# Layer 0 experts of a two-layer block: the 64-feature chunk's way down as products over 64 partitions, and both token halves' way down at the end of the step

## The chip, the cores and the metric

The kernel runs on one core of one Trainium2 chip. The metric is the time on the device, in microseconds (us). The core has a matrix engine (TensorE, PE in the profile; its weight loads are PEld), a vector engine (VectorE, DVE), a scalar engine for activation functions (ScalarE, ACT), a general engine (GpSimd, POOL) and an engine that here only issues transfers (SyncE, SP). PE reads SBUF and writes PSUM, which has eight banks; a bank holds 512 numbers of 4 bytes on each of 128 partitions. Everything is computed in 4-byte floats.

## The reference

The input x has shape (4, 512, 256): 2048 tokens of 256 features. Two layers follow each other; each adds an attention branch and a feed-forward branch to x. The change lies in layer 0's feed-forward branch, a gated MLP of 704 hidden features with a low-rank correction by the two best of eight experts:

```python
gate_base = xf @ Wg.T                       # 2048 x 704
up_base   = xf @ Wu.T
base_out  = silu(gate_base) * up_base @ Wd.T
# expert_w: the two largest of softmax(xf @ Wr.T) over 8 experts, else 0
for e in range(8):
    h = silu(gate_base + 2 * xf @ Ag[e].T @ Bg[e].T) * (up_base + 2 * xf @ Au[e].T @ Bu[e].T)
    acc += 2 * h @ Ad[e].T @ Bd[e].T * expert_w[:, e]
out = base_out + acc
```

Layer 0's other branch is a gated recurrent attention (mLSTM) with an MLP of 1024 features; layer 1 has softmax attention over the four batch rows and an MLP with 2-of-4 sparsity. The change does not touch them.

## The kernel before

**Tiling.** The 512 positions are cut in four blocks of 128 (step j = 0 to 3); a block holds 4 x 128 = 512 tokens. `experts(j)` computes the branch above for one block, in two token halves of T = 256 tokens. The 704 features are five chunks of 128 and one of 64. For a chunk and a half, one PSUM bank holds the gate (256 columns) and the up product (256 columns) of 128 features. `products(ps, parts, step)` adds to that bank: step 0 is the base product, steps 1 and 2 add the low-rank terms of the first and the second chosen expert. After each step `gated` makes silu(gate) x up from the bank: ACT's Silu into `sl`, then DVE's product into `hid` (step 0) or into `he` (steps 1 and 2). A bank must have been read before the next step may add to it.

**The 64-feature chunk.** It is done once for both halves (`pair`): half 0's 64 features lie on partitions 0 to 63 of the bank and half 1's on 64 to 127. On the way in, the two halves' products therefore use 64 columns of the PE array each and stand side by side (records with 128*64). The results `hb["pair"]` and `he[0]` (named `he_pair`) have both halves, one above the other.

**The way back.** There are two. The delta: `dps[half]`, a PSUM tile `acc` of 512 columns, sums `adT` x `he` over the chunks; `finish` multiplies it by the routing weights (`tmp`) and adds the two slots to `dw`. The way down: `add_down` sums, over the five chunks, the pair and `dw`, the products of `hid` with `wdT` and of `dw` with `bdT` into one bank `yp` per half, 128 tokens by 256 features twice, and DVE adds it to x. For the pair, `adT` and `wdT` hold the 64 features' rows twice: once on partitions 0 to 63 with zeros below (for half 0), and once on 64 to 127 with zeros above (for half 1). So a product over all 128 partitions of the pair takes only one half's features. POOL writes the zeros at the start (line 370).

**Order of the work.** No engine's order is written out by hand. Every piece of work is a Python generator (a stream); `Flow` runs the stream that is due first by the model `Clock`, which holds a time for each engine, an estimate for each instruction and which PSUM bank is free when. What comes out is a fixed program order for each engine (`InOrder`, line 216, records nearly all operations, so nearly all rows of the profile have that line). `flow.wait` gives control away until something is ready by the model; the hardware's own waits are set by semaphores as the data need them. Beside `experts(j)` run `front(j+1)` (layer norm, transposes, v and gates: `pt`, `vp`), `routing(j+1)` (`lp`, `spread`, `low`), `mlstm(j)` (`q_ps`, `k_ps`, `h_ps`, `r_ps`, `t_ps`, `qk`, `hp`, `o_ps`, then `w_out` and a norm) and `mlp(j-1)` (`gp`, `up`, `w_down`). In step 0 there is no MLP yet. `experts(j+1)` waits with its fourth chunk, and `mlp` with its fifth, for `mixed`, which is set when the step's way down is done.

**PSUM.** Seven banks are shared by all streams (`mm_ps`); the eighth belongs to `acc`. So half 1's delta may begin only when half 0's has been read, and half 0's way down is let into the order then, while half 1's chunks run.

Of the kernel before, what the change touches and what calls it, by code (L numbers as in the profile page):

```python
# [8 lines left out]
F32 = mybir.dt.float32  # L9
AF = mybir.ActivationFunctionType  # L10
ALU = mybir.AluOpType
AX = mybir.AxisListType

P = 128
B, S, D = 4, 512, 256
# [4 lines left out]
DFF = 704  # L20
# [5 lines left out]
AH, ADH = 16, 16  # L26
LOWEST = -3.0e38
FAR = 3.0e4


@with_exitstack
def layers_kernel(ctx: ExitStack, tc: tile.TileContext, io: dict, out: bass.AP):
# [17 lines left out]
    class Clock:  # L50
# [6 lines left out]
        def __init__(self):  # L57
            self.free = dict.fromkeys(("pe", "dve", "act", "pool", "sp", "dma"), 0.8)
            self.spans, self.before, self.rings = {}, {}, {}
            self.banks, self.held = [None] * 7, set()  # L60
            self.table = self.array = None
            self.stalls = []

# [14 lines left out]
            return max(max(s[2], s[3]) for s in spans)  # L78

        def take_bank(self, t):  # L80
            i = min(range(7), key=self.bank_free)
            name = t[:].tensor.name
            if self.banks[i] is not None:
                self.before[name] = self.banks[i]
            self.banks[i] = name

        def room(self, n):

            return sorted(self.bank_free(i) for i in range(7))[n - 1]


        def part(self, ap):
# [95 lines left out]
    def new(pool, shape, tag, bufs=None, dtype=F32):  # L188
        count[0] += 1
        kw = {} if bufs is None else {"bufs": bufs}  # L190
        t = pool.tile(shape, dtype, tag=tag, name=f"{tag}_{count[0]}", **kw)
        clock.ring(t, (id(pool), tag), bufs or (2 if tag in ("xn", "xnT") else 1))
        return t

    def mm_ps(name):
        count[0] += 1
        t = psum.tile([P, 512], F32, tag="mm", bufs=7, name=f"{name}_{count[0]}")
        clock.take_bank(t)
        return t

    def acc_ps():
        return new(psum, [P, 512], "acc", 1)

    class InOrder:

# [83 lines left out]
    def mm(out, lhsT, rhs, start, stop, at_once=1, **kw):  # L289
        array = (lhsT.shape[0], n_of(lhsT))  # L290
        us = 2 * max(0.107, n_of(rhs) * 0.00084) / at_once + 0.1 * (array != clock.array)
        clock.array = array
        clock.issue("pe", "matmul", (out, lhsT, rhs), {}, us)
        pe.matmul(out, lhsT, rhs, start=start, stop=stop, **kw)
# [13 lines left out]
    def load(t, src, by="sp"):  # L308
        dma(t, src, n_of(t) * t.shape[0] * 4 / 0.3e6, by)
        return t  # L310

    def weight(name, n, tag=None, width=None, by="sp"):

        d = io[name]
        kk = d.shape[0] // P
        t = new(wts, [P, width or kk * n], tag or name)[:, 0 : kk * n].rearrange(
            "p (k n) -> p k n", n=n)
        return load(t, d.rearrange("(k p) n -> p k n", p=P), by)
# [35 lines left out]
    for n, name in enumerate(("WgT", "WuT")):  # L354
        load(wguT[:, n, :, :], io[name].rearrange("(k p) n -> p k n", p=P))
    w_og = weight("w_og", D)
    lora = new(wts, [P, 2 * DFF + (NFC + 1) * E * R], "lora")
    bgT = load(lora[:, 0:DFF], io["BgT"])
    buT = load(lora[:, DFF : 2 * DFF], io["BuT"])
    load_x(1)  # L360
    adT = lora[:, 2 * DFF :].rearrange("p (c n) -> p c n", c=NFC + 1)
    wdT = new(wts, [P, NFC + 1, D], "WdT")
    for t, name in ((adT, "AdT"), (wdT, "WdT")):

        whole = DFF // P
        load(t[:, 0:whole, :], io[name][0 : whole * P, :].rearrange("(k p) n -> p k n", p=P))
        for half in range(2):
            mine = slice(half * P // 2, (half + 1) * P // 2)
            other = slice((1 - half) * P // 2, (2 - half) * P // 2)
            nc.gpsimd.memset(t[other, whole + half, :], 0.0)  # L370
            load(t[mine, whole + half, :], io[name][whole * P : DFF, :])
    bdT = load(new(wts, [P, D], "BdT"), io["BdT"])
    mh_c = column("mh_w")
    w_out = weight("w_out", D)
# [98 lines left out]
    with ExitStack() as l0:  # L473
# [5 lines left out]
        def tmp():  # L479
            return new(wk0, [P, 512], "tmp", 7)  # L480
# [410 lines left out]
        def add_down(xb, bp, terms):  # L891

            yield from flow.wait(banks=1)
            yp = mm_ps("yp")
            for i in range(2):
                for n, (a, lo, w) in enumerate(terms):
                    if n % 4 == 0 and i == 0:
                        yield from flow.wait(*(t[0] for t in terms[n : n + 4]))
                    elif n % 4 == 0:
                        yield 0  # L900
                    mm(yp[:, i * D : (i + 1) * D], a[:, lo + i * P : lo + (i + 1) * P], w,
                       start=(n == 0), stop=(n == len(terms) - 1))
            xv = xb[:, bp : bp + 2, :].rearrange("p b d -> p (b d)")
            dve.tensor_tensor(xv, yp, xv, ALU.add)
# [64 lines left out]
        def experts(j):  # L969
# [12 lines left out]
            def slots(t):  # L982
                return t.rearrange("p (s n) -> p s n", s=K_TOP)

            def here(half):
                return slice(half * T, (half + 1) * T)
# [42 lines left out]
                    yield flow.soon(0.2)  # L1029

            rooms, hb, he, dps = {}, {}, {}, {}
            ended = set()

            def finish(half, t):
                yield from flow.wait(dps[half])
                dve.tensor_tensor(t, dps[half], t, ALU.mult)
                dw = new(wk0, [P, T], "dw", 1)
                dve.tensor_tensor(dw, slots(t)[:, 0, :], slots(t)[:, 1, :], ALU.add)
                ended.add(half)
                terms = [(hb[half, c], 0, wdT[:, c, :]) for c in range(last)]  # L1040
                yield from add_down(
                    xb, 2 * half, [*terms, (hb["pair"], 0, wdT[:, last + half, :]), (dw, 0, bdT)])
                if half == 1:
                    mixed.add(j)

            def base(i):
                yield from flow.wait(xnT, *(wguT[:, m, :, :] for m in range(2)), banks=1)
# [20 lines left out]
            for i in range(len(order) + 4):  # L1068
                if i < len(order) and i not in rooms:
                    yield from base(i)  # L1070

                    while j not in lows and len(rooms) < 4:
                        yield from base(len(rooms))
                    while j not in lows:
                        yield flow.soon()
                    low, wT = lows[j]
                if i == len(order) - 1:
                    based.add(j)
                if i == 3:
                    while j > 0 and j - 1 not in mixed:  # L1080
                        yield flow.soon()
                for step in (1, 2):
                    n = i - step
                    if not 0 <= n < len(order):
                        continue
                    if step == 1:
                        he[n] = new(wk0, [P, 512], "he_pair") if n == 0 else tmp()
                    yield from unread(n)
                    yield clock.over(rooms[n])
                    yield clock.ready(*(low[m][:, step - 1, :] for m in range(2)))  # L1090
                    products(rooms[n], order[n], step)
                    gated(n, rooms[n], slots(he[n])[:, step - 1, :])
                    if step == 2:
                        flow.add(freed(n))
                        if n == len(order) - 1:
                            spent.add(j)
                n = i - 4
                if 0 < n < len(order):
                    _, half, c = order[n][0]
                    if c == 0:  # L1100
                        while half == 1 and 0 not in ended:
                            yield flow.soon()
                        dps[half] = acc_ps()
                        weight = tmp()
                        for s in range(K_TOP):
                            dve.tensor_scalar(
                                slots(weight)[:, s, :], wT[:, here(half)],
                                (-LORA_SCALE, LORA_SCALE)[s], 0.0, ALU.mult, ALU.max)
                        yield clock.over(dps[half])
                    yield from unread(n)  # L1110
                    yield clock.ready(he[n])
                    mm(dps[half], adT[:, c, :], he.pop(n), start=(c == 0), stop=False)
                    if c == last - 1:
                        yield from unread(0)
                        yield clock.ready(he[0])
                        mm(dps[half], adT[:, last + half, :], he[0], start=False, stop=True)
                        flow.add(finish(half, weight), after=True)

        def main():
            for j in range(NJ):  # L1120
# [36 lines left out]
        flow.until(lambda: not flow.streams)  # L1157


    qkvT = weight("qkvT", 3 * D, "WdT", (NFC + 1) * D)  # L1160
    f_gate = weight("f_gate", FF, "wguT", 4 * DFF)
    f_up = weight("f_up", FF, "lora", 2 * DFF + (NFC + 1) * E * R)
    f_down = weight("f_down", D, "w_gate")
    aoT = weight("aoT", D, "w_out")

# [221 lines left out]
```

## Time and profile before

| | |
|---|---|
| median of 3 runs | 798.95 us (798.55 to 799.13) |
| the profiled execution | 798.61 us |
| its span, first to last instruction | 796.9 us |
| PE busy | 779.3 us (98%) |
| DVE, ACT, POOL busy | 409.1, 258.1, 166.1 us |
| granted TensorE clock | 1.00 throughout |
| layer 0 to layer 1 | about 560 us into the span |

A row of a group has the line, engine, operation, the tile written and the tiles read, the shape, how often, and then busy time and the mean duration of one. For a matmul, "128*128" are partitions and columns of the PE array that it uses. A matmul of 4-byte floats appears as two records. Records of matmuls overlap, so their pace is read from start to start. A row in order of time has the start and the duration of a run of equal records, and in brackets how long the engine had stood idle before it and for whom. A row of waits has who waited for whom, the sum, how often, and the longest.

### The profile page before, as it was taken

Reading aid. Unit: us, or ns where it says so; the run is one execution under the profiler, and the core shown is the slowest. Engines: PE = TensorE matmul, PEld = TensorE weight load, DVE = VectorE, ACT = ScalarE, POOL = GpSimd, SP = SyncE. Lnnn points to the kernel's source line nnn. Section 1 sums busy time; section 2 is a strip of 40 time slices with the busy share of each in tenths; the row PEclk is TensorE's granted clock in tenths of the full one; section 3 lists DMA queues with packets and bytes.
Section 4 is the critical chain, followed back from the end, with each engine's and each line's share of the span. In section 5 each row is a group of like instructions: output and inputs, shape, how many; then the busy total and the mean of one; then the engine's idle time right before and its main releaser. Section 6 shows DMA issues by size and latency. Waiting matters only on the chain.

```text
span 796.9 us, 8736 instructions
## 1 busy us (share of the span) xinstructions
PE 779.3 (98%) x3334; PEld 536.2 (67%) x3334; DVE 409.1 (51%) x943; ACT 258.1 (32%) x462; POOL 166.1 (21%) x153
## 2 busy tenths in 40 slices
PE   6999999999999999999999999999999999999998
PEld 3678776876657687864778876655645485664486
DVE  5685545773531676452156433221256883975870
ACT  3454316461231545212156212111243405224310
POOL 5230160600510240060011040000233213342000
PEclk9999999999999999999999999999999999999999
DMA  8820000200000300000030012001000000000000
GB/s 264 275 75 1 1 0 13 96 1 1 0 1 0 107 1 1 1 0 1 0 107 1 1 67 92 1 0 53 0 1 0 1 18 10 1 24 4 0 27 27
DMA packets 18938, 25.37 MB, mean 32 GB/s; under 512 B 2768, under 2 KB 12752, under 8 KB 18896
## 3 DMA queue, kind: packets, MB, share of 16 engines
q1 hardware_dynamic: 17776, 24.27, 9.4%
q10 hardware_dynamic: 1120, 0.54, 0.2%
q8 instruction: 26, 0.43, 0.2%
q14 instruction: 16, 0.13, 0.1%
HBM read 22.65 MB, written 2.16 MB: 31 GB/s over the span
## 4 chain that ended last, share of the span: by engine, by line
PE 96%; DVE 2%; ACT 1%; issue 1%; POOL 0%; POOLq 0%; DVEq 0%; ACTq 0%
PE yp L216 24%; PE chunk L216 19%; PE gp L216 14%; PE up L216 14%; PE acc L216 5%; PE qk_ps L216 3%; PE hp L216 3%; PE pt L216 2%; PE vp L216 2%; PE o_ps L216 2%; PE v_ps L216 2%; PE lp L216 2%; PE qk L216 1%; PE q_ps L216 1%; PE h_ps L216 1%; PE st_ps L216 1%
## 5 line engine op out<-in xcount | busy, mean ns | idle before, releaser
L216 PE MATMUL chunk<-low,lora 128*128 128x256 f32 (+1 forms) x384 | 87.4, 385 | 2.8 <-DVE tmp L216 2.8
L216 ACT ACTIVATE sl<-chunk 128x256 f32<-128x256 f32 x132 | 48.3, 384 | 120.3 <-PE chunk L216 113.0
L216 PE MATMUL chunk<-xnT,wguT 128*128 128x256 f32 (+1 forms) x384 | 84.2, 383 | 0.0
L216 PEld LDWEIGHTS chunk<-xnT,wguT 128*128 128x128 f32 (+1 forms) x384 | 63.7, 181 | 17.7 <-issue 6.0
L216 PEld LDWEIGHTS chunk<-low,lora 128*128 128x128 f32 (+1 forms) x384 | 63.1, 181 | 17.7 <-issue 4.0
L216 ACT ACT_TABLE_LOAD x44 | 56.5, 1283 | 21.1 <-PE chunk L216 15.8
L216 DVE TENSOR_TENSOR hid<-up,tmp 128x512 f32<-128x512 f32 x32 | 22.1, 691 | 78.1 <-PE up L216 75.4
L216 PE MATMUL gp<-featT,w_gate 128*128 128x512 f32 x128 | 60.2, 593 | 0.0
L216 PE MATMUL gp<-xnT,wguT 128*128 128x512 f32 x128 | 60.2, 592 | 0.0
L216 PE MATMUL up<-featT,w_up 128*128 128x512 f32 x128 | 60.2, 592 | 0.0
L216 PE MATMUL up<-xnT,lora 128*128 128x512 f32 x128 | 60.1, 592 | 0.0
L216 DVE TENSOR_TENSOR x<-yp,x 128x512 f32<-128x512 f32 x24 | 16.6, 691 | 83.3 <-PE yp L216 83.3
L216 PE MATMUL yp<-w_gate,hs 128*128 128x256 f32 x256 | 56.2, 379 | 0.0
L216 PE MATMUL yp<-w_down,hid 128*128 128x256 f32 x256 | 56.1, 379 | 0.0
L216 PEld LDWEIGHTS yp<-w_down,hid 128*128 128x128 f32 x256 | 48.6, 190 | 8.3 <-issue 1.7
L216 PEld LDWEIGHTS yp<-w_gate,hs 128*128 128x128 f32 x256 | 48.6, 190 | 6.6
L216 ACT ACTIVATE tmp<-gp 128x512 f32<-128x512 f32 x32 | 19.1, 597 | 101.3 <-PE gp L216 101.3
L216 PE MATMUL yp<-WdT,hid 128*128 128x256 f32 x192 | 46.3, 384 | 0.0
L216 PEld LDWEIGHTS up<-xnT,lora 128*128 128x128 f32 x128 | 24.3, 190 | 29.8 <-issue 29.7
L216 PEld LDWEIGHTS gp<-featT,w_gate 128*128 128x128 f32 x128 | 24.2, 190 | 28.8 <-issue 28.2
L216 PEld LDWEIGHTS up<-featT,w_up 128*128 128x128 f32 x128 | 24.1, 190 | 27.5 <-issue 27.3
L216 PEld LDWEIGHTS gp<-xnT,wguT 128*128 128x128 f32 x128 | 23.9, 190 | 27.4 <-issue 26.5
(198 smaller groups left out, 1211.3 us busy)
## 6 DMA issues: line engine op xcount, KB each, us to landing
ct<-m_dram SPq DMA_DIRECT2D x8, 1024.0 KB, 8.0
out<-x SPq DMA_DIRECT2D x8, 256.0 KB, 2.1
x<-in_x SPq DMA_DIRECT2D x3, 512.0 KB, 10.1
w_gate<-in_w_gate SPq DMA_DIRECT2D x1, 1024.0 KB, 6.0
w_up<-in_w_up SPq DMA_DIRECT2D x1, 1024.0 KB, 7.3
w_down<-in_w_down SPq DMA_DIRECT2D x1, 1024.0 KB, 10.7
wguT<-in_f_gate SPq DMA_DIRECT2D x1, 1024.0 KB, 4.9
lora<-in_f_up SPq DMA_DIRECT2D x1, 1024.0 KB, 5.0
```

The lines of the kernel that those rows point to most:

```text
L216: return tc.keep_in_program_order(f(*args, **kw))
```

## The change

`adT` and `wdT` lose the sixth slice and the zeros: the 64 features' rows stand twice in one slice, on partitions 0 to 63 and on 64 to 127. The products with the pair take 64 partitions each, half 0's on the upper and half 1's on the lower, issued one directly behind the other and written to two banks. For the delta this means that `dps[0]` and `dps[1]` must be open at once: the private bank goes, all eight are shared, half 0's delta ends with the pair, and half 1's begins with it. For the way down both halves' banks `yps` are taken together after half 1's delta. Half 0's `finish` only makes its `dw` (two buffers now); half 1's does the pair for both halves, then half 0's chunks and `dw`, then half 1's. `mixed` is set at the same place, the end. The routing weights are scaled after a half's last chunk instead of before its first. The scheduler makes a new order from this for every engine.

```diff
+BANKS = 8
...
-    def acc_ps():
-        return new(psum, [P, 512], "acc", 1)
...
-    adT = lora[:, 2 * DFF :].rearrange("p (c n) -> p c n", c=NFC + 1)
-    wdT = new(wts, [P, NFC + 1, D], "WdT")
+    adT = lora[:, 2 * DFF :].rearrange("p (c n) -> p c n", c=NFC)
+    wdT = new(wts, [P, NFC, D], "WdT")
     for t, name in ((adT, "AdT"), (wdT, "WdT")):
         whole = DFF // P
         load(t[:, 0:whole, :], io[name][0 : whole * P, :].rearrange("(k p) n -> p k n", p=P))
         for half in range(2):
-            mine = slice(half * P // 2, (half + 1) * P // 2)
-            other = slice((1 - half) * P // 2, (2 - half) * P // 2)
-            nc.gpsimd.memset(t[other, whole + half, :], 0.0)
-            load(t[mine, whole + half, :], io[name][whole * P : DFF, :])
+            load(t[half * P // 2 : (half + 1) * P // 2, whole, :], io[name][whole * P : DFF, :])
...
             def finish(half, t):
                 yield from flow.wait(dps[half])
                 dve.tensor_tensor(t, dps[half], t, ALU.mult)
-                dw = new(wk0, [P, T], "dw", 1)
+                dw = dws[half] = new(wk0, [P, T], "dw", 2)
                 dve.tensor_tensor(dw, slots(t)[:, 0, :], slots(t)[:, 1, :], ALU.add)
-                ended.add(half)
-                terms = [(hb[half, c], 0, wdT[:, c, :]) for c in range(last)]
-                yield from add_down(
-                    xb, 2 * half, [*terms, (hb["pair"], 0, wdT[:, last + half, :]), (dw, 0, bdT)])
-                if half == 1:
-                    mixed.add(j)
+                if half == 0:
+                    return
+                yield from flow.wait(banks=2)
+                yps = [acc() for _ in range(2)]
+
+                def down(half, i, a, w, stop=False, **kw):
+                    mm(yps[half][:, i * D : (i + 1) * D], a[:, i * P : (i + 1) * P], w, stop=stop,
+                       skip_group_check=True, **{"start": False, **kw})
+
+                for i in range(2):
+                    for half in range(2):
+                        down(half, i, hb["pair"][mine[half], :], wdT[mine[half], last, :],
+                             start=(i == 0), at_once=2)
+                for half in range(2):
+                    for i in range(2):
+                        yield 0
+                        for c in range(last):
+                            down(half, i, hb[half, c], wdT[:, c, :])
+                    yield from flow.wait(dws[half])
+                    for i in range(2):
+                        down(half, i, dws[half], bdT, stop=(i == 1))
+                    xv = xb[:, 2 * half : 2 * half + 2, :].rearrange("p b d -> p (b d)")
+                    dve.tensor_tensor(xv, yps[half], xv, ALU.add)
+                    released(yps[half])
+                mixed.add(j)
...
-                    mm(dps[half], adT[:, c, :], he.pop(n), start=(c == 0), stop=False)
-                    if c == last - 1:
-                        yield from unread(0)
-                        yield clock.ready(he[0])
-                        mm(dps[half], adT[:, last + half, :], he[0], start=False, stop=True)
-                        flow.add(finish(half, weight), after=True)
+                    mm(dps[half], adT[:, c, :], he.pop(n), start=((half, c) == (0, 0)),
+                       stop=((half, c) == (1, last - 1)))
+                    if c < last - 1:
+                        continue
+                    if half == 0:
+                        yield from unread(0)
+                        yield from flow.wait(he[0], banks=1)
+                        dps[1] = acc()
+                        for h in range(2):
+                            mm(dps[h], adT[mine[h], last, :], he[0][mine[h], :], start=(h == 1),
+                               stop=(h == 0), at_once=2)
+                    weight = tmp()
+                    for s in range(K_TOP):
+                        dve.tensor_scalar(
+                            slots(weight)[:, s, :], wT[:, here(half)],
+                            (-LORA_SCALE, LORA_SCALE)[s], 0.0, ALU.mult, ALU.max)
+                    released(dps[half])
+                    flow.add(finish(half, weight), after=True)
```

## The prediction

> **What bounds the kernel now.** I read the page first, then TensorE's waits, its groups with their shapes kept apart, and its instructions in order of time.
>
> ```profile
> span 796.9 us, 8736 instructions
> ...
> PE 779.3 (98%) x3334; PEld 536.2 (67%) x3334; DVE 409.1 (51%) x943; ACT 258.1 (32%) x462; POOL 166.1 (21%) x153
> ```
>
> TensorE (PE) is idle for 796.9 - 779.3 = 17.6 us. Who is waited for:
>
> ```profile
> PE pt L216 <- DVE xn L216: 7.6, 1, 7.6
> PE chunk L216 <- DVE tmp L216: 2.8, 3, 1.5
> PE hp L216 <- DVE ct L216: 1.6, 2, 0.9
> PE h_ps L216 <- ACT qs L216: 1.3, 3, 0.5
> PE yp L216 <- ACT oT L216: 0.2, 1, 0.2
> ```
>
> That is 13.5 us; the other 4 lie behind the last product. 7.6 us are the start. So the time is the sum of PE's work plus some 6 us of small waits, and only these two can move. The groups that the change touches:
>
> ```profile
> L216 PE MATMUL yp<-WdT,hid 128*128 128x256 f32 x192 | 46.3, 384 | 0.0
> ...
> L216 PE MATMUL acc<-he_pair,lora 128*128 128x512 f32 x16 | 8.4, 608 | 0.0
> ```
>
> A matmul makes two records. The 384 and 608 ns are latencies; what counts is the pace, from start to start. In the first stretch below, eight records of `chunk<-xnT,wguT` at 256 columns take 305.89 - 304.17 = 1.72, so 0.216 a record. At 512 columns it is 0.43 (`acc`, two records from 304.17 back to 303.31).
>
> ```profile
> 304.17 1.89 PE L216 MATMUL chunk<-xnT,wguT 128*128 128x256 f32 x8
> 305.89 1.03 PE L216 MATMUL chunk<-low,lora 128*128 128x256 f32 x4
> 306.85 1.17 PE L216 MATMUL qk<-qm,kT 32*128 32x128 f32 x32
> 307.95 1.13 PE L216 MATMUL chunk<-low,lora 128*128 128x256 f32 x4
> 308.92 0.97 PE L216 MATMUL hp<-va,ct 128*128 128x33 f32 x8
> ```
>
> ```profile
> 118.18 1.89 PE L216 MATMUL chunk<-xnT,wguT 128*128 128x256 f32 x8
> 120.00 1.08 PE L216 MATMUL chunk<-low,lora 128*64 128x256 f32 x8
> 121.01 1.99 PE L216 MATMUL chunk<-xnT,wguT 128*128 128x256 f32 x8
> 122.84 1.04 PE L216 MATMUL pt<-ident,xn 128*128 128x128 f32 x8
> ```
>
> These show how small products run side by side: `qk` (32 partitions, four at once, each into its own bank) does 32 records in 1.10 us, and the pair chunk (64 columns of the array, two at once) does 8 in 1.01, where one after the other they would need 3.5 and 1.73. They also show what a change of the array's shape costs, if the groups on both sides are counted in. First stretch: 308.92 - 305.89 = 3.03, against 2 x 0.864 for the `chunk` groups and 0.87 for eight slots of 128 columns (the eight transposes from 59.80 to 60.67): 0.43 over. Second: 4.66 against 1.73 + 0.86 + 1.73: 0.34 over.
>
> **The change, part by part.** (1) Delta of the 64-feature chunk, `acc<-he_pair`. Removed per step j: two products over 128 partitions, half of them zeros, 4 records x 0.43 = 1.72. Added: two over 64 partitions side by side, 2 slots x 0.43 = 0.86. (2) Its way down, `yp<-WdT`: removed four products, 8 x 0.216 = 1.73; added four over 64 partitions in two banks, 4 slots = 0.86. No row shows 64 partitions x 128 columns. The bounds of the price of such an excursion are 0.34 (columns split) and 0.43 (partitions split); I take 0.43, since `qk` splits partitions and loads 128 columns of weights per tile as the new products do. So each group gains 0.864 - 0.43 = 0.43, and four steps of two groups gain 3.5 us.
>
> Here the Trainium skill speaks against the row. Page "TensorE: Matmul & The Clock Gate", section "Measured speedup vs the span model", has 3.07x for four row tiles at 512 columns, 77% of the ideal. For two tiles I estimate 1.53x from that: 3.45 us a step become 2.25, a gain of 1.2, or 4.8 us in all. Page "TensorEngine Tiling (Array Packing)", section "Key Properties", says that a change of the tiling mode drains the array: a price per excursion, not per column. The trace agrees with that one and gives its size (0.43 around `qk`, whose tiles otherwise keep the pace of one). My groups are short and stand alone, so I take the trace: 3.5.
>
> (3) In the built order, two new groups stand directly beside another split group: in step 0 the way down follows `chunk` of the pair (64 columns), in step 1 it follows `qk`. One change of shape is saved in each, about half of 0.43: 0.4 us together (bounds 0 and 0.86). PE's work: -3.9 us.
>
> (4) Half 0's whole way down is moved behind half 1's last delta: 24 records of WdT, 4 of BdT (28 x 0.216 = 6.05 us of PE work, of which the pair's part is priced above), and DVE's `x<-yp,x` of 0.69. The amount is the same, but it was filler between `hp` and `qk` and is now missing there; experts chunks stand there instead. Worked out against the built order:
>  - Step 1, after `qk`. `hp` waited 0.86 and 0.76 because it stood right behind `qk`; now `gp` (1.72) and nine WdT products (over 3 us) stand between. Gain 1.6.
>  - Tail of step 0. The wait of 1.54 at 97.46 was for DVE's gated product, late because ACT ran the tanh of `o_ps` and a Square of 0.95 before the Silu. `o_ps` now comes after the tail, with `hp` among the chunks. From the `qk` before, DVE has four `ct` (2.6), a `tmp<-pr` and the gating (0.42 each) plus hand-overs, about 3.8 us; PE has 1.94 + 0.86 + 0.81 = 3.6, and a second such place is about as close. I charge 0.4 and gain 1.54.
>  - Behind `yp<-w_out` of step 0, the way down (4.3 us of cover in the old order) is gone: PE reaches the pair's second low-rank product 1.07 + 1.83 + 0.86 = 3.8 us later, while DVE does `xn` (0.69), a gate (0.42), four statistics (0.53 each) and two small ones before `he_pair` (0.42): 4.3, plus 0.2 to hand over. New wait 0.7. Queued behind it on PE: step 1's chunks, and the transposes of `xn`.
>  - Step 1 between `r_ps` and `t_ps`: the layer norm of the next row block now stands ahead on DVE (three statistics 1.7, four small ops 0.7) of `tmp<-chunk`, for which PE's low-rank product waits: about 0.75.
>  - Half 0's `x` addition (0.69) now stands on DVE ahead of `ss`, which POOL's `qm` (2.34) and the transposes `pt<-ident,qm` wait for. `qm` is ready about 16.3 us after `spread` ends (o_ps 3.45, tanh, Square, reduction, POOL's 5.44 us power, `ss`, `qm`); PE has 16.9 us of work before it. Hidden by half 1's ten WdT products; without them 0.7.
> Waits: -3.2 + 1.9 = -1.3 us. Steps 2 and 3 have MLP products as filler around the change and the same order from `q_ps` to `t_ps`: nothing.
>
> (5) The four memsets on POOL (0.80 to 1.89 us) go, so `ident` is ready 1.1 us earlier. Nothing is won: DVE's first statistics start at 3.38, when the first x lands (issued 0.80, fastest landing 2.6). If x came earlier, 0.5. SP's loads keep number, sizes and order, except that two loads for layer 1 change places; the last of them is issued at 487 and layer 1's products read from 565 on. The second `dw` buffer and the eighth shared bank are not a cost: one bank was the delta's own, and two are held only at the end of a step. The masks' scaling (`tmp<-wT`, 0.29 each) moves behind the deltas; `dw` is read ten products later.
>
> Sum: -3.9 - 1.3 = -5.2 us on the profiled execution of 798.61 (span 796.9 and 1.7 around it): 793.4. The median of the runs shown is 0.34 above that execution: 793.8.
>
> **The rivals.** (a) *The waits just go*: the four new waits don't come. -3.9 - 3.2: 791.8; with excursions at 0.34, 0.7 less, 791.1. For it: with over 98% busy, the planner found cover nearly everywhere. Against: the two DVE queues above. (b) *The waits come back elsewhere*: new waits eat all of the 3.2 and half of the gain in work: about 797. For it: steps 0 and 1 have little filler, and the old order had three waits for gating there. (c) *No overlap*: products over 64 partitions go one after the other. The work stays, excursions cost 8 x 0.43 - 0.4, the waits win 1.3: 800.7. Against: `qk` overlaps four tiles, 6 to 7 ns apart in start. (d) *Slower, the filler is missing*: in step 0 no MLP runs yet, and the way down of half 0 covered `ct<-qk` on DVE (0.68 each, 15.2 us waited in all) between `hp`. The chunks in its place need ACT and DVE (0.38 + 0.42) for each product and DVE is in their way. If all 6.05 us are uncovered in step 0 and half in step 1, 9.1 us: 802.9. It is slower than before once more than 5.2 us beyond my 1.9 stay uncovered. Against: the order puts 8 products of chunks and `lp` (3.4 us) there, and the waits that I find are below 1 us.
>
> **How the numbers follow.** Forecast 0.46, (a) 0.17, (b) 0.17, (c) 0.07, (d) 0.13. What a measurement can tell from no change is 0.2%, 1.6 us: faster is below 797.35, slower above 800.55. Faster: forecast, (a) and (b), 0.80. (c) lies at the upper edge and is halved, and of (d) a third ends within: same 0.07, slower 0.13. Range: from (a) at 0.34 an excursion, 791.0, to 798.0 past (b); the outside is (c), (d) and little else.
>
> **What would show it.** PE's busy time near 775.5 us; `he_pair` records in twos 6 ns apart and the group with its neighbours at 1.3 us against 1.72; no wait of `hp` for `ct`; waits for `tmp` and `he_pair` of about 2 to 3 us in all (with the 0.63 and 0.68 at 35 and 58, whose order is unchanged); 7.6 at the start. Wrong if the new groups take as long as the old, or if PE's idle time in the first 250 us grows by more than 3 us.

## The result, and the profile after

| | before | after |
|---|---|---|
| median | 798.84 us (798.28 to 799.81) | 792.87 us (792.41 to 793.17) |
| the profiled execution | 798.61 us | 792.43 us |
| its span | 796.9 us | 790.7 us |
| PE busy | 779.3 us | 775.3 us |
| PE idle in the span | 17.6 us | 15.4 us |

The ratio of the times is 0.9923, with a 95% interval of 0.9911 to 0.9936: the changed kernel is faster by 6.0 us. The granted TensorE clock is 1.0 in both.

The page of the changed kernel, its span and its busy times:

```profile
span 790.7 us, 8729 instructions
...
PE 775.3 (98%) x3334; PEld 530.7 (67%) x3334; DVE 407.4 (52%) x943; ACT 260.6 (33%) x464; POOL 166.6 (21%) x149
```

The span is 6.2 us shorter. PE's busy time gives 779.3 - 775.3 = 4.0 of it, PE's idle time 17.6 - 15.4 = 2.2. PE is still the bound at 98%.

PE's waits after: who waited for whom, the sum, how often, the longest.

```profile
PE pt L214 <- DVE xn L214: 7.8, 1, 7.8
PE h_ps L214 <- ACT qs L214: 1.5, 3, 0.5
PE chunk L214 <- DVE tmp L214: 1.3, 2, 0.7
PE st_ps L214 <- issue: 0.4, 1, 0.4
PE yp L214 <- ACT oT L214: 0.2, 1, 0.2
PE chunk L214 <- DVE he_pair L214: 0.2, 1, 0.2
```

The wait of `hp` for `ct` (1.6 us in all) is gone, and of the three waits of `chunk` for `tmp` the longest, 1.5. Two small ones are new: `st_ps` and `he_pair`. The sum is 11.4 us, against 13.5.

PE's groups with their shapes kept apart, the two that now use 64 partitions (line, engine, tiles, shape, records | busy us, mean ns | idle before):

```profile
L214 PE MATMUL acc<-WdT,hid 64*128 64x256 f32 x32 | 4.5, 402 | 0.0
L214 PE MATMUL acc<-he_pair,lora 64*128 64x512 f32 x16 | 4.5, 641 | 0.0
```

The number of records is the same, 192 for the way down and 16 for the delta; 32 and all 16 of them now use 64 partitions. The delta's 8.4 us of busy time are 4.5; each record is longer (641 ns against 608), but they overlap in twos.

What such a group costs is read from start to start. Step 1's delta in order of time:

```profile
165.58 1.02 PE L214 MATMUL acc<-tmp,lora 128*128 128x512 f32 x2
166.53 1.13 PE L214 MATMUL acc<-he_pair,lora 64*128 64x512 f32 x4
167.59 1.99 PE L214 MATMUL chunk<-xnT,wguT 128*128 128x256 f32 x8
169.42 1.89 PE L214 MATMUL chunk<-low,lora 128*128 128x256 f32 x8
```

From 165.58 to 169.42 it is 3.84 us. At full pace the three groups need 0.86 (two records at 0.43), 0.86 (two slots at 0.43) and 1.73 (eight records at 0.216), 3.45 together. So the excursion to 64 partitions costs 0.39: about 0.09 before the group, 0.20 within it and 0.10 behind it.

### The profile page after: what moved, and what is told of

Same layout as the page of the kernel before. It is cut to its first block, busy times and chain, and to the rows that moved or that the text cites. A ratio compares the mean times of both kernels' runs of the same rounds, so it can differ in the third digit from the quotient of the medians.

```text
span 790.7 us, 8729 instructions
## 1 busy us (share of the span) xinstructions
PE 775.3 (98%) x3334; PEld 530.7 (67%) x3334; DVE 407.4 (52%) x943; ACT 260.6 (33%) x464; POOL 166.6 (21%) x149
## 4 chain that ended last, share of the span: by engine, by line
PE 95%; DVE 2%; issue 1%; ACT 1%; DMA 0%; POOL 0%; DVEq 0%; ACTq 0%
PE chunk L214 18%; PE yp L214 18%; PE gp L214 14%; PE up L214 14%; PE acc L214 11%; PE qk_ps L214 3%; PE hp L214 3%; PE pt L214 2%; PE vp L214 2%; PE o_ps L214 2%; PE lp L214 2%; PE v_ps L214 2%; PE qk L214 1%; PE q_ps L214 1%; PE st_ps L214 1%
## 5 line engine op out<-in xcount | busy, mean ns | idle before, releaser
L214 DVE TENSOR_TENSOR x<-yp,x 128x512 f32<-128x512 f32 x16 | 11.0, 690 | 68.9 <-PE yp L214 68.9
L214 PE MATMUL acc<-WdT,hid 128*128 128x256 f32 (+1 forms) x192 | 41.3, 386 | 0.0
```

Of the source, the lines that this page charges most:

```text
L214: return tc.keep_in_program_order(f(*args, **kw))
```

## The experiments

E1, E2 and E4 have the instructions of the changed kernel in the same order (E4 but for the order of four products), so they separate what the products do from what the order does.

**E1: the order alone.** Every product with the pair goes over 128 partitions again. The stationary rows are the 64 features' twice, so it also adds the other half's features; only the amount of work is meant. `rows` tells the planner to reckon with 64, so that it makes the same order.

```diff
-    def mm(out, lhsT, rhs, start, stop, at_once=1, **kw):
-        array = (lhsT.shape[0], n_of(lhsT))
+    def mm(out, lhsT, rhs, start, stop, at_once=1, rows=None, **kw):
+        array = (rows or lhsT.shape[0], n_of(lhsT))
...
-                        down(half, i, hb["pair"][mine[half], :], wdT[mine[half], last, :],
-                             start=(i == 0), at_once=2)
+                        down(half, i, hb["pair"], wdT[:, last, :],
+                             start=(i == 0), at_once=2, rows=P // 2)
...
-                            mm(dps[h], adT[mine[h], last, :], he[0][mine[h], :], start=(h == 1),
-                               stop=(h == 0), at_once=2)
+                            mm(dps[h], adT[:, last, :], he[0], start=(h == 1),
+                               stop=(h == 0), at_once=2, rows=P // 2)
```

> The changed kernel with every engine's order kept instruction for instruction, but the products with the pair over all 128 partitions again (each takes the features of both halves, so this part of the result is another; only the time is read). It separates the new order from the products side by side. Theory (the side-by-side products save 0.864 us less some 0.40 for the change of the array's shape, twice a step, with 0.4 us more where two shapes adjoin: about 4.0 us; the new order gives the other 2 us in waits): 796.8 us, PE busy near 779.3, waits as in the changed kernel (11.4 us). Rival 1 (the order does it all, the products gain nothing): 792.9. Rival 2 (the order gives nothing, the products all 6 us): 798.8.

Measured: 796.54 us (796.45 to 797.52), against 798.86 before on the same chip; ratio 0.9972 (0.9961 to 0.9983). PE's busy time is 779.2 us, that of before, and its waits are those of the changed kernel (7.9, 1.5, 1.3, 0.4, 0.2 and 0.2 us).

So the new order is worth 798.86 - 796.54 = 2.3 us with no product narrowed, and narrowing them is worth 796.54 - 792.87 = 3.7 (the kernel before took 798.86 and 798.84 us beside the two).

**E2: the delta narrowed, the way down not.** Of E1's edit, only the way down's part.

> As before, but only the pair's way down over 128 partitions; the delta stays over 64 (the way down takes the features of both halves, another result for this part; only the time is read). Order kept. Theory (each group gains its 0.864 less the price of one change of shape, and the way down gains 0.4 more in the two steps where it stands beside another split group): delta 4 x 0.46 = 1.85, way down 4 x 0.46 + 0.4 = 2.25, so 792.87 + 2.25 = 795.1 us. Rival (the price per change is so high for the short way down that only the delta gains): 793.0. Rival (the longer products of the delta gain nothing): 796.8.

Measured: 794.84 us (793.96 to 795.73), ratio 0.9945 (0.9932 to 0.9958). By the medians the delta is worth 796.54 - 794.84 = 1.7 us, the way down 794.84 - 792.87 = 2.0.

**The same sums without the start.** A median of five or six executions carries the start of the program with it, and the start varies. The same 16 `vp` products, in the changed kernel's profile and in E2's:

```profile
9.97 5.08 PE L214 MATMUL vp<-wvg,xnT 128*128 128x280 f32 x16
10.09 6.19 PE L214 MATMUL vp<-wvg,xnT 128*128 128x280 f32 x16
```

The first of these records follow each other every 0.467 us, the later ones every 0.236. The pace changes at about 12.1 us in the one and 14.5 us in the other, where the trace's record of the granted clock goes to 1.0. Behind that, a kernel repeats itself closely. From the first `spread` to the start of the last group (`yp<-w_gate,hs`, 64 records), with the later experiments beside:

| profile | us |
|---|---|
| before | 757.34 |
| E1 | 755.21 |
| E2 | 753.13 |
| changed kernel; E10 (the same kernel again); E4 | 751.03; 751.03; 751.04 |
| E3 | 752.46 |
| E6 | 755.60 |
| E7; E11 (the same kernel again) | 749.92; 749.91 |
| E9 | 748.56 |

So the order is worth 2.1 us, the delta 2.1 and the way down 2.1, together 6.3. The medians' 1.7 for the delta is low by less than the start can move a single execution (`vp` takes 4.82 us in E1's profile and 6.19 in E2's).

**E4: does the order within a group matter?** The way down issues half 0's two products with the pair, then half 1's two, where the changed kernel alternates. Neighbours in the program then use the same 64 partitions.

```diff
-                for i in range(2):
-                    for half in range(2):
+                for half in range(2):
+                    for i in range(2):
```

> The changed kernel with the four products of the pair's way down in another order: both of half 0's first, then both of half 1's, so that a product has a neighbour on the other 64 partitions only at the seam. If records start strictly in order (theory), half 0's second record pair holds back half 1's first: of 8 records only those at the seam overlap, 7 places instead of 4, 3 x 0.216 = 0.65 us a step, 2.6 us in all: 795.5 us. If PE starts whatever has its 64 partitions free (rival), 792.9. In between, 794.2, if one matmul's two records can be passed by the next matmul's.

Measured: 792.62 us (792.01 to 793.27), ratio 0.9922 (0.991 to 0.9934): as fast as the changed kernel. The theory behind 795.5, products started strictly in the program's order, falls. In E4's order of time, step 2:

```profile
334.32 5.66 PE L214 MATMUL acc<-WdT,hid 64*128 64x256 f32 x28
339.81 1.03 PE L214 MATMUL acc<-BdT,dw 128*128 128x256 f32 x4
```

and in the changed kernel's:

```profile
334.49 5.65 PE L214 MATMUL acc<-WdT,hid 64*128 64x256 f32 x28
339.97 1.03 PE L214 MATMUL acc<-BdT,dw 128*128 128x256 f32 x4
```

A row is named by its first record's shape, so `64*128 ... x28` is eight records of the pair and twenty of half 0's chunks. From its start to `BdT` it is 5.49 and 5.48 us. Half by half in strict order, the two halves could only have met at the seam, seven slots in place of four: 0.65 us more. In the single records of E4 they start in twos all the same, 14 ns apart, four times. The records don't show which 64 partitions they use; that the two of each pair lie on different halves is inferred from the time that the group takes.

**E3: the price of an excursion.** The pair's products for the second 128 tokens come later, behind half 0's chunks for the first: the same products, one trip to 64 partitions and back more in each step.

```diff
-                for i in range(2):
+                def pair_down(i):
                     for half in range(2):
                         down(half, i, hb["pair"][mine[half], :], wdT[mine[half], last, :],
                              start=(i == 0), at_once=2)
+                pair_down(0)
                 for half in range(2):
                     for i in range(2):
                         yield 0
                         for c in range(last):
                             down(half, i, hb[half, c], wdT[:, c, :])
+                        if (half, i) == (0, 0):
+                            pair_down(1)
```

> The pair's way down of each step is divided: its products for the first 128 tokens of each half come first as before, those for the second 128 come behind half 0's five chunks for the first. TensorE so goes over to 64 partitions and back once more in each of the four steps; the number and the length of the products stay. If a trip costs by itself, 0.40 us as measured where the pair's products stand in the changed kernel, the time is 792.9 + 4 x 0.40 = 794.5. If the 0.40 belongs to the place and not to the trip (the first products of a group waiting for something else), it is 792.9.

Measured: 794.57 us (793.99 to 794.85), ratio 0.9945 (0.9933 to 0.9958). That is 1.7 us above the changed kernel, 0.43 a trip; without the start 752.46 - 751.03 = 1.4, 0.36 a trip. The waits are the same (11.3 us), PE's busy time is 776.9 against 775.3. The same place in E3's order of time:

```profile
335.41 6.05 PE L214 MATMUL acc<-WdT,hid 64*128 64x256 f32 x28
341.29 1.03 PE L214 MATMUL acc<-BdT,dw 128*128 128x256 f32 x4
```

28 records take 5.88 us here and 5.48 there: 0.40. The price belongs to the trip, not to the number of products. It also says where narrowing stops to pay: two products of 256 columns side by side save 0.43 us and cost about 0.40.

**E6: is it the held-back way down that removes the waits?** The delta as changed; each half's way down by `add_down` over 128 partitions as soon as its `dw` is there, as before.

```diff
+                terms = [(hb[half, c], 0, wdT[:, c, :]) for c in range(last)]
+                yield from add_down(
+                    xb, 2 * half, [*terms, (hb["pair"], 0, wdT[:, last, :]), (dw, 0, bdT)])
-                if half == 0:
-                    return
-                yield from flow.wait(banks=2)
-                yps = [acc() for _ in range(2)]
...
```

> The pair's delta as in the changed kernel (64 partitions, side by side, both halves at the end of half 0), the way down as in the kernel before: each half's own products over 128 partitions as soon as its weights are there, half 0's between half 1's chunks. (The rows of the pair's way down hold both halves' features here, so the sum that it makes is not the layer's.) By the other runs the delta side by side is worth 1.7 us, so 797.1 if all of the order's 2.3 us comes from holding half 0's way down back to the end, and 794.9 if it comes from moving the delta product of half 1 away from the tail. Theory: the tail's 1.5 us goes with the delta, the two waits of hp for ct stay: 795.6 to 796.2.

The edit also moves the scaling of the routing weights back ahead of a half's first chunk.

Measured: 797.12 us (796.35 to 797.98), ratio 0.9979 (0.9971 to 0.9987). The theory falls, and the first alternative holds: of the 1.8 us gained, 1.7 are the delta's, and the order gives nothing (without the start E6 gains 1.7, less than the delta's 2.1). The tail of step 0 in E6:

```profile
91.08 3.62 PE L214 MATMUL o_ps<-w_og,xnT 128*128 128x256 f32 x16
94.54 1.89 PE L214 MATMUL chunk<-low,lora 128*128 128x256 f32 x8
96.27 1.02 PE L214 MATMUL acc<-tmp,lora 128*128 128x512 f32 x2
98.83 1.13 PE L214 MATMUL chunk<-low,lora 128*128 128x256 f32 x4 [1.54 <-DVE tmp L214]
```

It is the wait of before, of the same length, though the pair's delta has left the tail. In the changed kernel the low-rank products of the last chunks come before `o_ps`:

```profile
82.32 0.98 PE L214 MATMUL hp<-va,ct 128*128 128x33 f32 x8
83.13 1.11 PE L214 MATMUL chunk<-low,lora 128*128 128x256 f32 x4
84.07 1.02 PE L214 MATMUL acc<-tmp,lora 128*128 128x512 f32 x2
```

With half 0's way down held back, the planner had nothing else to put between the `hp` groups and put the last chunks there. What used to stand there becomes the filler behind `o_ps`, and PE waits for none of it. The place of the scaling isn't what does it: E7 below scales ahead of the first chunk in step 0, holds the way down back, and has no wait in the tail. One reservation: the planner gives E6 another order in step 1 too, so E6 shows what the tail's wait depends on, not what each `hp` wait does; there one of the two came back (0.8 us).

**E5: one trip per step.** Can the price be paid once? Half 0's delta stays open until the end of half 1; there both halves' products with `he_pair` and the pair's way down stand together.

```diff
-                    mm(dps[half], adT[:, c, :], he.pop(n), start=((half, c) == (0, 0)),
-                       stop=((half, c) == (1, last - 1)))
-                    if c < last - 1:
+                    mm(dps[half], adT[:, c, :], he.pop(n), start=(c == 0), stop=False)
+                    if (half, c) != (1, last - 1):
                         continue
...
+                    yield from unread(0)
+                    yield from flow.wait(he[0], banks=2)
+                    yps = [acc() for _ in range(2)]
+                    for h in range(2):
+                        mm(dps[h], adT[mine[h], last, :], he[0][mine[h], :], start=False,
+                           stop=True, at_once=2)
+                    for b in range(2):
+                        for h in range(2):
+                            down(yps, h, b, hb["pair"][mine[h], :], wdT[mine[h], last, :],
+                                 start=(b == 0), at_once=2)
```

> Half 0's delta is kept open until half 1's end, so that the pair's two delta products and its four products of the way down stand together: one change of the array's shape a step instead of two (the masks' scaling for both halves at half 1's last chunk). Theory (price of a change 0.40 us): four changes fewer, 1.6 us, but in two steps the way down loses its neighbour of another split shape or gains one (0.2 each way): 791.3 us, if the waits stay. In its order step 0 has three groups of hp directly behind qk, where PE should wait for ct on DVE (4 x 0.68 us): 0.8 to 1.5 us back, so 792.1 to 792.8. Rival (the price of a change is small and the gain of the changed kernel was less overlap than order): 793 to 794.5.

Measured: 793.58 us as a median, ratio 0.9933 (0.9914 to 0.9952), but the six times are two values: 791.83, 791.65, 791.31 with a mean granted clock of 1.0, and 795.60, 795.33, 795.68 with 0.996. The lower value lies between the two that were expected; the upper was expected by nobody. The profiled execution is one of the upper. PE's order of time there, in step 0:

```profile
81.19 1.17 PE L214 MATMUL qk<-qm,kT 32*128 32x128 f32 x32
83.13 3.87 PE L214 MATMUL hp<-va,ct 128*128 128x33 f32 x24 [0.76 <-DVE ct L214]
86.81 2.05 PE L214 MATMUL chunk<-low,lora 128*128 128x256 f32 x4
88.65 3.34 PE L214 MATMUL acc<-tmp,lora 128*128 128x512 f32 x4
```

and the same time in two stretches (the stretch, its length, the busy time and instructions of PE, PEld, DVE, ACT and POOL, then the granted clock, the DMA share and GB/s):

```profile
81.35:84.76 3.41, 2.65 (x47) 2.46 (x47) 2.38 (x4) 0.00 (x0) 0.00 (x0) 1.00 0.00 0
84.76:91.59 6.83, 6.83 (x20) 4.88 (x20) 4.27 (x16) 0.39 (x1) 1.84 (x3) 0.50 0.00 1
```

For 6.8 us TensorE runs at half its clock: four `chunk` records take 1.84 us in place of 0.86. Half of 6.8 is 3.4 us lost, and the two values lie 795.6 - 791.65 = 3.9 apart; the other 0.5 is within what the start moves. Ahead of the fall stand four things in a row: `qk` on 32 partitions, a wait of 0.76, and three `hp` groups of 33 columns each, which the changed kernel has apart, with wide products between.

**E8: a wide product ahead of each `hp` group.** E5, with a product that nothing reads put before step 0's last four `hp` groups.

```diff
                 hp = mm_ps("hp")
+                if first and s == 1:
+                    mm(hp[:, D : 2 * D], wq[:, 0, :], w_og[:, 1, :], start=True, stop=True)
```

> The one-trip kernel with a useless product of 256 columns over 128 partitions ahead of each of step 0's last four hp groups (it writes columns of the bank that nothing reads). It adds 4 x 0.43 = 1.7 us of products and covers up to 0.8 us of the first hp's wait. If three hp groups of 33 columns in a row are what halves the granted clock, it stays at 1.0 in every execution and the time is 791.6 + 1.7 - 0.8 = 792.5, up to 793.3, without a second value. If the clock falls for another reason (the wait, the phase of the step, a power limit that large products raise), about half of the executions are 4 us longer again, at 796 to 797.

Measured: 794.25 us, 793.62 to 794.41 in five executions, ratio 0.994 (0.9926 to 0.9953), with a clock of 0.999 or more in each. There is no second value, as expected. The time is 1 us above the upper end of the expectation: the added product waited for `ct` as well and covered nothing, and the planner moved other work about.

```profile
83.16 0.70 PE L214 MATMUL hp<-w_og,wq 128*128 128x256 f32 x2 [0.77 <-DVE ct L214]
83.69 0.97 PE L214 MATMUL hp<-va,ct 128*128 128x33 f32 x8
84.50 0.68 PE L214 MATMUL hp<-w_og,wq 128*128 128x256 f32 x2
```

and the 3.4 us around the first of them, in the form of E5's stretches:

```profile
81.50:84.92 3.42, 2.65 (x44) 2.39 (x41) 2.51 (x5) 0.00 (x0) 0.00 (x0) 1.00 0.00 0
```

Only two `hp` groups follow the wait here before a chunk, not three. So `qk` and the wait alone don't bring the clock down; the kernel before, with `qk` and a wait of 0.86 us in step 1, says the same. PE's busy share isn't what decides either: it is 2.65 us in this stretch as in E5's stretch just before the fall.

**E7: the mixed kernel.** Step 0 with two trips, steps 1 to 3 as in E5; in step 0 a half's masks are scaled with its first chunk.

```diff
+                    if j == 0:
+                        if (half, c) == (0, 0):
+                            yield from flow.wait(banks=1)
+                            dps[0] = acc()
+                        if c == 0:
+                            weight = tmp()
...
+                        continue
```

> Step 0 close to the changed kernel (two trips to 64 partitions), steps 1 to 3 with one trip: half 0's delta stays open, and both halves' last delta products and the pair's way down stand together at the end of half 1. Three trips fewer at 0.40 each, and no three hp groups in a row in step 0: 792.9 - 1.2 = 791.7, at a granted clock of 1.0 throughout. If one-trip steps lose as much again to late masks, 792.9; if the clock falls here too, 795 to 796 in some executions.

Measured: 791.65 us (790.81 to 792.23), ratio 0.9909 (0.9896 to 0.9923), the clock at 0.999 or more in each. As expected.

**E9, E10, E11: the clock once more, and the lead.** E9 is E7 with half 0's and half 1's masks in step 0 scaled one chunk later (`if c == 1`), which gives another order in step 0. E10 is the changed kernel, E11 is E7, all on one chip.

> The mixed kernel with half 0's masks scaled one chunk later, which moves step 0's products: three hp groups of 33 columns stand in a row again, but a chunk and a delta product of full width stand between the qk group and them. If three hp groups in a row halve the granted clock, it falls in about half of the executions and the time has two values about 4 us apart (792 and 796). If it takes the narrow qk group, the wait and the three hp groups together, the clock is 1.0 in every execution and the time is one value, 791.5 to 793.

> The changed kernel beside the mixed one on the same chip: 792.9, and so 1.2 us above the mixed kernel if that one's lead is real, equal to it if the lead came from the chip.

> The mixed kernel once more, beside the changed one on the same chip: 791.7.

Measured: E9 790.93 us (789.91 to 791.02), ratio 0.9897 (0.9883 to 0.991); E10 792.45 (791.95 to 793.15), ratio 0.9919; E11 791.39 (791.22 to 791.99), ratio 0.9907. E9's step 0:

```profile
75.52 1.17 PE L214 MATMUL qk<-qm,kT 32*128 32x128 f32 x32
76.62 1.13 PE L214 MATMUL chunk<-low,lora 128*128 128x256 f32 x4
77.59 1.02 PE L214 MATMUL acc<-tmp,lora 128*128 128x512 f32 x2
78.45 2.76 PE L214 MATMUL hp<-va,ct 128*128 128x33 f32 x24
```

The same 24 records of `hp` take 2.76 us and not 3.87, and all four executions have one value and a clock of 0.999 to 1.0. So three `hp` groups alone don't bring the clock down either, as far as four executions tell: with a fall in half of them, as in E5, four without one would come by chance once in sixteen times. The second reading fits: E5, the only kernel whose clock fell, has `qk`, the wait and the three groups close together. Whether it takes all three was not separated.

E9 and E11 are both faster than the changed kernel, by 1.5 and 1.1 us (2.5 and 1.1 without the start). None of E9's executions overlaps with one of E10's five; of E11's, the slowest (791.99) lies just above E10's fastest (791.95). E9 is the best version found: 8.1 us below before on that chip. Its PE waits are 7.8, 1.5, 0.6 and 0.2 us, 10.1 in all; beside the saved trips it has lost one of the two waits for `tmp`, that of `st_ps` and that of `he_pair`.

## Why the prediction was right

793.8 us were forecast, 792.87 measured. The likeliest case came, with the time about halfway between it and rival (a).

- **(1), (2) and (3), PE's work.** -3.9 forecast; -4.0 in the busy times, -3.7 by E1's median, -4.2 without the start. The way down with its two neighbours: 2.1 forecast, 2.0 by the median, 2.1 without the start. The delta: 4 x 0.43 = 1.7 forecast and 1.7 by E2's median, but 2.1 without the start, so the median's agreement is luck. The price of an excursion was taken from a row of another shape (`qk`, 0.43). Between full-width products it is 0.39 to 0.40; beside `hp`, where three of the four deltas stand, it is less. In step 0, from the `hp` before the delta to the chunk behind it, E1 takes 75.25 - 71.83 = 3.42 us and the changed kernel 74.86 - 71.98 = 2.88: 0.54 gained of 0.86, a price of 0.32. Why it is lower there stays open. The rule with which the trace was weighed, of the Trainium skill's page "TensorE: Matmul & The Clock Gate", "Measured speedup vs the span model", would have given 4.8; as a factor on the products it doesn't fit, since inside the group two tiles keep the pace of one. "TensorEngine Tiling (Array Packing)", "Key Properties", has the right form, a cost per change of mode, and E3 gives its size.
- **(3), the neighbours.** In step 0 the pair chunk (64 columns), the way down (64 partitions) and their surroundings cost 0.55 over the pace; two separate trips would be 0.34 + 0.39 = 0.73. So 0.2 is saved there, as forecast, and E1 has the same for step 1, where the way down follows `qk`: it takes 0.66 us more than the changed kernel's in steps 0 and 1 and 0.47 in steps 2 and 3. Step 0 of the changed kernel:

```profile
96.62 1.02 PE L214 MATMUL acc<-tmp,lora 128*128 128x512 f32 x2
97.58 1.95 PE L214 MATMUL chunk<-xnT,wguT 128*64 128x256 f32 x16
99.45 5.65 PE L214 MATMUL acc<-WdT,hid 64*128 64x256 f32 x28
104.94 1.03 PE L214 MATMUL acc<-BdT,dw 128*128 128x256 f32 x4
```

- **(4), the waits that go.** -3.2 forecast; both `hp` waits (0.86 and 0.76) and the tail's 1.54 are gone, -3.2. In the kernel before, the tail's and the longer `hp` wait were:

```profile
97.46 1.13 PE L216 MATMUL chunk<-low,lora 128*128 128x256 f32 x4 [1.54 <-DVE tmp L216]
170.95 1.05 PE L216 MATMUL hp<-va,ct 128*128 128x33 f32 x8 [0.86 <-DVE ct L216]
```

E6 confirms the tail's reason in so far as the wait of the same length stays where half 0's way down isn't held back.
- **(4), the waits that come.** This is the term that was mis-sized: +1.9 forecast, about +0.95 found. Tail of step 0: 0.4 forecast, none. `he_pair`: 0.7 forecast, 0.17. Between `r_ps` and `t_ps`: 0.75 forecast, 0.36, seen as eight records that take 2.09 us for 1.73. And one that was not forecast, 0.42 at `st_ps`. The profile names PE's own issue for it (E4's and E8's name POOL's `ct`), but `st_ps` reads `qs`, and ACT's copy of that, late behind a table load, ends at 155.00:

```profile
153.00 1.28 ACT L214 ACT_TABLE_LOAD   x1
154.43 0.57 ACT L214 COPY qs<-kt_ps 128x512 f32<-128x512 f32 x1
155.10 2.02 PE L214 MATMUL st_ps<-wv,qs 128*128 128x264 f32 x8 [0.42 <-issue]
```

In the kernel before, the copy ended at 144.22 and `st_ps` came at 146.02 with other products between. So -3.2 + 0.95 = -2.2 for the profiled pair, -2.3 by E1's median, -2.1 without the start, and -1.3 forecast. The waits for `tmp` and `he_pair` are 1.5 us in all, below the 2 to 3 named as a sign.

The reason why the first two are smaller is in DVE's order of time. Behind `qk` in step 0:

```profile
77.96 2.48 DVE L214 TENSOR_TENSOR ct<-qk,ct 128x512 f32<-128x512 f32 x4 [0.55 <-PE qk L214]
80.36 0.42 DVE L214 TENSOR_TENSOR tmp<-pr 128x256 f32<-128x256 f32 x1
80.69 0.42 DVE L214 TENSOR_TENSOR hid<-chunk,sl 128x256 f32<-128x256 f32 x1
```

and before `he_pair`:

```profile
117.24 0.69 DVE L214 TENSOR_TENSOR xn<-yp,xn 128x512 f32<-128x512 f32 x1 [1.03 <-PE yp L214]
117.85 0.41 DVE L214 TENSOR_TENSOR hid<-chunk,sl 128x256 f32<-128x256 f32 x1
...
120.70 0.42 DVE L214 TENSOR_TENSOR he_pair<-chunk,sl 128x256 f32<-128x256 f32 x1
```

The forecast added durations (0.42 for a gate, 0.69 for `xn`). From start to start a gate takes 0.33 and `xn` 0.61. The first queue, from the end of `qk` at 77.94 to the end of the gate at 81.11, is 3.2 us and not 3.8, and the product that needs it started at 81.37 with 0.26 to spare. The second is 117.24 to 121.12, 3.9 and not 4.3, against PE's 117.13 to 121.00. With PE the prediction had used the pace; with DVE it didn't.
- **(4), `x` ahead of `ss`.** Hidden, as forecast: `pt<-ident,qm` of step 0 has no wait.
- **(5).** The start has 7.8 us against 7.6; nothing is won by dropping the memsets, as forecast.
- **The rivals.** (a) was 1.1 us too low, (b) 4 us too high. (c), no overlap, is excluded by the records in twos and by E1; (d) by the waits. Both terms, work and waits, came out larger than forecast, so no error hid another. About half of the new waits came, which is why the time lies between the forecast and (a).

## What to carry to other kernels

Products over half of the array pay by the group, not by the product: on this kernel a trip to another tile shape and back costs 0.3 to 0.4 us, about as much as two side-by-side products of 256 columns save. Put all of a step's narrow products together, next to other narrow ones if there are any (E7 and E9). When a queue of DVE is laid against PE's, add start-to-start times on both. When PE is the bound and has to wait for a chain of small operations, look for work with no fresh input that can be held back to stand there: here an order alone was worth 2.3 of 6.0 us by the medians, 2.1 of 6.3 without the start.

## What the runs showed of the hardware that was not expected

- **The clock can fall with PE hardly idle.** In the profiled execution of E5 the granted clock is 0.50 from 84.76 to 91.59 us, and three of six executions have the longer time, 3.9 us of 792. The Trainium skill's "TensorE: Matmul & The Clock Gate", "Part 1: The HAM clock gate", tells of an activity window of about 3.4 us that runs freely, and of a fall after an idle one. On the window the traces agree: in each one's record of the clock, every stretch at full clock and E5's at half lasts a whole multiple of 3.413 us (E5: 71.680 to the fall, then 6.827; the others 774.8 to 785.1), and the first change comes at 11.7 to 14.5 us of the span. On the idleness they don't: PE is busy for 2.65 of the 3.41 us just before E5's fall, which hold `qk`, the wait and `hp` alone. The stretch at the same place of E8's count, 81.50 to 84.92, has two of the added wide products in it; that of the kernel before in step 1, 168.99 to 172.40, has `qk`, the wait and `hp` for 2.8 us and then 0.6 of `yp`. The clock fell in neither, so some 0.6 us of wide products were enough to hold the clock. That rests on one profile of each kernel; that E5's three fast executions had another phase is argued, since none of them was profiled.
- **Products start out of program order, it seems, when their partitions are free.** E4 issues two products on the same 64 partitions, then two on the other 64: the records still start in twos, and the group takes 5.49 us against 5.48.
- **Two tiles of 64 partitions at full pace.** Inside a group a pair of records takes 0.21 us at 256 columns, what one record over 128 partitions takes; the loss is at the borders of the group.
- **TensorE's start varies.** In the thirteen profiles the first `vp` group takes 4.82 to 6.19 us, while the rest of a kernel repeats within 0.01 us (751.03, 751.03 and 751.04 us above).
